# Cross-attention, eight sequences, one core: the queries of batch 2 by seven Strassen products too, weight sums in another order, and parts of GpSimd's work on VectorE and ScalarE

## The chip, the core and the metric

The kernel runs on one core of a Trainium2 chip. The core has five engines that run side by side: TensorE (PE in the profile; its loads of weights are PEld), VectorE (DVE), ScalarE (ACT), GpSimd (POOL) and SyncE (SP), which issues nearly all the transfers. Each engine works through its own list of instructions in order; where one needs another engine's result, it waits on a semaphore, and all that stands behind it on that engine waits too. The metric is the device time of one execution in microseconds.

## The reference

Eight sequences of 256 tokens with 1024 features attend to eight contexts of 256 tokens, with 32 heads of 32 features. Everything is float32, and the mask is all true.

```python
x = (hidden - mu) * rsqrt(var + 1e-5) * gamma + beta     # over the 1024 features
Q = split_heads(x @ Wq.T)
K = V = split_heads(memory)                              # no projection
probs = softmax(where(mask, Q @ K^T * 32 ** -0.5, -inf))
out = hidden + merge_heads(probs @ V) @ Wout.T
```

So there are two large products for each batch, x @ Wq.T and attn @ Wout.T, each of 256 x 1024 by 1024 x 1024, and between them the scores, the softmax and the weighted values of 32 heads.

## The kernel before

**Slots.** The main loop (`for n in range(N)`) has N = 64 passes, called slots here: eight batches of eight groups of four heads. In slot n TensorE computes the scores of group n+1 (`scores`), the values of group n-2 (`values`), a part of the queries of a later batch, and a part of the output projection of the batch before (`project_steps`). In the same slot VectorE, ScalarE and GpSimd work on the softmax of group n+1 (`softmax_parts`). So the first scores instruction of group n+1 marks where slot n begins on TensorE. Slot 4 begins at 50.87 us of the profile, slot 5 at 58.41, slot 6 at 66.17, slot 7 at 73.71, slot 8 at 81.25, slot 9 at 88.79, slot 10 at 96.30 and slot 11 at 103.83.

**The softmax of one group.** For each of four heads, `exps` has VectorE add the mask bias to the scores in PSUM and take the minimum, and ScalarE take the exponential with its sum. Then `normalize` takes the reciprocal of the sum on VectorE and scales the head's 2 x 256 values on GpSimd, `blocks` transposes them in blocks of 32 on VectorE, and `aside` copies two heads' part away on ScalarE for transfers between partitions (pT<-pT and pT<-pc). The order within a slot is written out: exponentials of heads 0, 1, 2, normalize 0, exponentials of 3, copies of queries, normalize 1, a fill, blocks 0, normalize 2, a fill, blocks 1, aside 0, normalize 3, a fill, blocks 2. The last transpose, the second aside and the transfers are the tail; in slots below 7 the tail runs inside the next softmax, after its first exponentials. The scores use four PSUM banks, all of one group, so the scores of group n+1 wait until VectorE has read those of group n.

**Queries.** Direct: `make_q` multiplies eight 128 x 128 blocks of wq by the transposed, normalized x of one batch (256 columns) for each of eight output chunks, and ScalarE copies each result out with the bias. `SPLIT` is the first batch whose queries are computed by seven products of half size instead (Strassen's scheme in Winograd's form): `query_product` does one product a slot, 16 matmuls of 128 columns, in seven of eight slots, and `copy_product` evacuates it on ScalarE (p = 0, 1, 2, 5: four instructions) or VectorE (p = 3, 4, 6). The eighth slot, the one in which the projection does seven steps, has none. The products take sums of quarters of x (`sum_x`, on GpSimd: S1 and S2 two slots before the first product, S4 one before, S3 later) and sums of quarters of wq (`sum_wq`, on GpSimd, made once: T1, T3, T2, T4). T1 to T4 share room with wq itself: some overwrite quarters of it, and T1, B11 and T3 take turns in a small tile, `ring`, which is filled from copies in DRAM (`keep_wq`, `load_ring`, through SP's queue). Before the change SPLIT is 3: batches 0 to 2 are direct.

**x on its way in.** The x of a batch from 2 on is loaded, measured (`ln_stats`: bn_stats, bn_aggr and an addition on VectorE, the power -0.5 on GpSimd), normalized on ScalarE (`ln_norm`), transposed in blocks on VectorE (`blocks_x`) and moved between partitions by sixteen transfers (`move_x`, xnT<-xe). For batch 2 the moves stand in slots 5, 6 and 7; for a later batch whose products begin in slot f they stand in slots f-6, f-5 and f-4. gamma is multiplied into wq, one output chunk a slot (`fold`, GpSimd, slots 0 to 7), since from batch 1 on x is moved without it.

**The projection** (`product_steps`) has seven products too, of four steps each: A11, A12, S2, S3, A22, S1, S4, with sums T1 to T4 of Wout (`sum_wo`, tile wo, on GpSimd). `STEPS` says how many steps stand at three places of each slot. A12 and S2 use the same PSUM bank one after the other (pool ps_o): S2 can begin when VectorE has added A12 to the residual (`store`, row L748), and that addition comes after GpSimd has added p1, the product A11, to the same residual (`add_p1`, row L739). Batch 0 has steps of its own:

```python
if b == 0:
    return STEPS[:1] + ((0, 6, 0), (0, 2, 0), (0, 4, 1), (0, 3, 1)) + STEPS[5:]
return STEPS     # ((0,0,0), (0,7,0), (0,1,2), (0,2,2), (0,2,1), (0,1,2), ...)
```

**GpSimd's order.** What GpSimd does in a slot besides normalizing comes behind it in program order: the power of `ln_stats`, sums for the projection and for x, folds, then the wo and wq sums of the table `sums`.

## Time and profile before

| | us |
|---|---|
| median of 3 runs (571.57 to 572.5) | 572.11 |
| the profiled execution's own time | 571.69 |
| its span in the profile | 569.9 |
| slots 9 to 17 on TensorE (88.79 to 168.66) | 79.87 |
| slots 25 to 33 on TensorE (228.28 to 304.57) | 76.29 |

| group | instructions | mean ns of one |
|---|---|---|
| L533, GpSimd scales half a head's values | 512 | 478 |
| L366, GpSimd multiplies gamma into a chunk of wq | 8 | 1900 |
| L182 and L396, GpSimd makes a quarter of a wo or wq sum | 16 and 16 | 1278 and about 1285 |
| L253, the second half of x 1 normalized on GpSimd | 1 | 3775 |
| L253, other halves of x normalized on VectorE | 2 | 800 |
| L332, moves of x, from issue to landing (50 to 95 us) | 16 | 2000 to 4800, median 3200 |

In the timelines below, the columns are the start in microseconds, the duration, the engine, the line, the operation, the tiles (written<-read), the shape and the number of instructions, and in brackets how long the engine had been idle and what ended the wait. In the groups by form they are the same names, then the busy time of all, the mean duration of one in ns, and the engine's idle time before them. Matmuls overlap, so a group's busy time divided by its number is the price of one, not its mean duration.

### The profile page before, as it was taken

To read this page: it belongs to the slowest core of one execution; us is meant where nothing else is said; L and a number is where in the kernel's file an instruction comes from. 1 tells how busy PE (TensorE), PEld (TensorE's weight loads), DVE (VectorE), ACT (ScalarE), POOL (GpSimd) and SP (SyncE) were. 2 spreads that over 40 slices of the span, in tenths; PEclk is the share of its full clock that TensorE was granted. 3 is DMA by queue.
4 is the path that set the end of the run, shared out by engine and by line. 5 is a ranking of instruction groups with operands and counts; after the bars stand their busy time and mean duration, and the time that the engine had idled before them with its cause. 6 is when DMAs were issued, how large, how long until landed. Compare 5 with 4: busy or idle time off the path is not lost.

```text
span 569.9 us, 20012 instructions
## 1 busy us (share of the span) xinstructions
PE 565.0 (99%) x7170; PEld 393.5 (69%) x7170; DVE 460.1 (81%) x1696; ACT 411.3 (72%) x1426; POOL 413.2 (72%) x679
## 2 busy tenths in 40 slices
PE   9999999999999999999999999999999999999997
PEld 8788786666667677667776777667866767755454
DVE  5888888787877878989898888988888878879823
ACT  4688887777768858787667867778767776769920
POOL 2788899899897896876568576677648657448780
PEclk9999999999999999999999999999999999999999
DMA  8974777656687767877688767896568874436751
GB/s 308 396 194 145 221 198 214 209 163 191 190 254 261 223 182 212 258 219 226 183 244 237 222 170 215 245 281 176 139 180 262 240 212 132 136 110 180 212 164 75
DMA packets 47187, 117.98 MB, mean 207 GB/s; under 512 B 8944, under 2 KB 9712, under 8 KB 47088
## 3 DMA queue, kind: packets, MB, share of 16 engines
q1 hardware_dynamic: 46944, 116.69, 68.8%
q8 instruction: 57, 0.93, 0.7%
q14 instruction: 42, 0.34, 0.2%
q10 hardware_dynamic: 144, 0.01, 0.0%
HBM read 65.28 MB, written 11.53 MB: 135 GB/s over the span
## 4 chain that ended last, share of the span: by engine, by line
PE 90%; POOL 3%; DVE 2%; ACT 2%; issue 1%; DMA 1%; SPq 1%; DVEq 0%; POOLq 0%; ACTq 0%
PE po_S L706 20%; PE pq_A L445 16%; PE pv L620 11%; PE sc L484 11%; PE pq L345 10%; PE po_A L706 10%; PE pq_S L445 6%; PE po_end L773 3%; POOL e L533 2%; ACT e L524 1%; PE po_last L773 1%; PE busy L119 1%; DVE e L520 1%; DMA pT<-pc 1%; POOL wo L182 1%
## 5 line engine op out<-in xcount | busy, mean ns | idle before, releaser
L533 POOL TENSOR_SCALAR e<-e,rden 128x256 f32<-128x256 f32 x512 | 236.0, 478 | 113.3 <-DVE rden L531 110.2
L524 ACT ACTIVATE e<-e,mn 128x256 f32<-128x256 f32 x512 | 254.0, 501 | 48.3 <-DVE mn L520 47.1
L539 DVE STREAM_TRANSPOSE pT<-e 128x512 f32<-128x512 f32 x256 | 180.9, 707 | 45.5 <-POOL e L533 34.8
L520 DVE CUSTOM_DVE_ANT_0 e<-sc,mb 128x256 f32<-128x256 f32 x512 | 185.3, 416 | 27.4 <-PE sc L484 26.8
L545 ACT COPY pc<-pT 128x512 f32<-128x512 f32 x128 | 79.1, 618 | 68.8 <-DVE pT L539 39.3
L524 ACT ACTIVATION_READ_ACCUMULATOR e<-e,mn 128x1 f32 x512 | 97.9, 191 | 0.0
L345 PE MATMUL pq<-xnT,wq 128*128 128x256 f32 (+1 forms) x368 | 84.0, 382 | 0.2 <-ACT qa L354 0.2
L345 PEld LDWEIGHTS pq<-xnT,wq 128*128 128x128 f32 x368 | 68.8, 190 | 14.8 <-issue 4.0
L706 PE MATMUL po_S<-wo,at 128*128 128x512 f32 x152 | 74.5, 607 | 0.4 <-DVE r L748 0.2
L484 PEld LDWEIGHTS sc<-k,qa 32*128 32x128 f32 x1024 | 46.1, 184 | 41.6 <-issue 24.6
L620 PE MATMUL pv<-pT,v 64*32 64x128 f32 x4096 | 74.2, 274 | 0.0
L484 PE MATMUL sc<-k,qa 32*128 32x256 f32 x1024 | 73.6, 400 | 0.1
L620 PEld LDWEIGHTS pv<-pT,v 64*32 64x32 f32 x4096 | 57.0, 105 | 22.5 <-issue 13.1
L706 PE MATMUL po_A<-wo,at 128*128 128x512 f32 x128 | 59.4, 605 | 0.0
L706 PE MATMUL po_S<-wo,s 128*128 128x512 f32 x104 | 49.9, 605 | 0.0
L531 DVE RECIPROCAL rden<-den 128x2 f32<-128x2 f32 x256 | 37.7, 147 | 6.3 <-ACT e L524 5.4
L520 DVE DVE_READ_ACCUMULATOR2_ANT mn<- 128x1 f32 x512 | 42.5, 83 | 0.0
L706 PEld LDWEIGHTS po_A<-wo,at 128*128 128x128 f32 x128 | 22.9, 189 | 25.7 <-issue 24.6
L445 PEld LDWEIGHTS pq_A<-xnT,wq 128*128 128x128 f32 x320 | 37.3, 192 | 4.8 <-issue 4.1
L706 PEld LDWEIGHTS po_S<-wo,at 128*128 128x128 f32 x152 | 25.6, 190 | 20.9 <-issue 19.3
L445 PE MATMUL pq_A<-xnT,wq 128*128 128x128 f32 x320 | 37.3, 275 | 0.0
L739 POOL TENSOR_TENSOR r<-r,p 128x512 f32<-128x512 f32 x24 | 30.7, 1278 | 3.6 <-ACT e L524 2.5
(101 smaller groups left out, 612.1 us busy)
## 6 DMA issues: line engine op xcount, KB each, us to landing
v<-in_kv_dram SPq DMA_DIRECT2D x32, 512.0 KB, 4.3
pT<-pT SPq DMA_DIRECT2D x128, 128.0 KB, 2.4
pT<-pc SPq DMA_DIRECT2D x128, 128.0 KB, 4.2
ring<-kept_T SPq DMA_DIRECT2D x18, 512.0 KB, 5.7
k<-in_kv_dram SPq DMA_DIRECT2D x32, 256.0 KB, 2.9
x<-in_x_dram SPq DMA_DIRECT2D x15, 512.0 KB, 6.1
r<-in_x_dram SPq DMA_DIRECT2D x28, 256.0 KB, 4.4
out_dram<-r SPq DMA_DIRECT2D x28, 256.0 KB, 3.3
```

Source lines behind the costliest of these rows:

```text
L345: nc.tensor.matmul(pqs[n], wq[:, o, c, :], xnTs[b](c), start=(c == 0), stop=(c == NC - 1),)
L445: nc.tensor.matmul(pqs[b][:, o, :], w[:, c], x_[:, c], start=begins and o + c == 0, stop=c == NK - 1, skip_group_check=True,)
L484: nc.tensor.matmul(scs[n][j][:, s, :], qa[r, n % NQ, ts(s, P)], ks[n - n % 2][r, n % 2, :], start=True, stop=True,)
L520: nc.vector.tensor_tensor_reduce(out=e[:, s, :], in0=pss[j][:, s, :], in1=mbs[n // NQ], scale=1.0, scalar=NO_SCORE, op0=ALU.add, op1=ALU.m ...
L524: nc.scalar.activation(e[:, s, :], e[:, s, :], AF.Exp, bias=mn[:, s : s + 1], scale=-1.0, accum_out=den[:, s : s + 1],)
L531: nc.vector.reciprocal(rden, dens[j])
L533: nc.gpsimd.tensor_scalar(es[j][:, s, :], es[j][:, s, :], rden[:, s : s + 1], 1.0, ALU.mult, ALU.mult,)
L539: nc.vector.transpose(pT[:, :, :, j, :, :].rearrange("p a i s k -> p (a i) s k"), es[j].rearrange("p s (b t) -> p b s t", t=K),)
L545: nc.scalar.copy(pc[:, :, ts(j, 2)], pT[:, 1, :, ts(j, 2)])
L620: nc.tensor.matmul(pvs[n][r][j * HD : (j + 1) * HD], vs[n - n % 2][ts(r, 2 * K), i, ds(n % 2 * P + j * HD, HD)], pT[ts(r, 2 * K), :, i, j, ...
L706: nc.tensor.matmul(po, operand(b, name)[:, c], wo[:, which, c], start=begins and c == 0, stop=c == NK - 1, skip_group_check=not begins,)
L739: nc.gpsimd.tensor_tensor(r, r, p1s[b], ALU.add)
```

## The change

SPLIT becomes 2, so batch 2's seven products stand in slots 10 to 16. Batch 0's projection takes the same steps as the other batches. The weight sums of wq are made in slots 6 to 14 in the order T1, T2, T3, T4, with T2 = B22 - T1 and T3 = T2 - B11; T3 is made in `ring` and kept from there. Batch 2's product A11 reads B11 from wq itself. Of GpSimd's work, these parts move: the last head's normalizing of softmaxes 1 to 14 to ScalarE (with its reciprocal and instruction ahead of `blocks(1)`), the second half of x 1 to VectorE, gamma into the second half of wq to VectorE (`fold_late`, eight instructions as fills of slots 4 and 5), and four wo sums and three wq sums to VectorE. The other wo sums stand in earlier slots. The moves of batch 2's x stay in slots 5 to 7.

```diff
--- before.py
+++ after.py
@@ -173,13 +173,13 @@
             wo[:, which, ts(pair, 2)], rows.rearrange("(c p) q -> p c q", c=2)
         )
 
-    def sum_wo(which, c):
+    def sum_wo(which, c, engine=nc.gpsimd):
 
         a, b, op = {
             T3: (B22, B12, ALU.subtract), T2: (T3, B11, ALU.add),
             T4: (B21, T2, ALU.subtract), T1: (B12, B11, ALU.subtract),
         }[which]
-        nc.gpsimd.tensor_tensor(wo[:, which, c], wo[:, a, c], wo[:, b, c], op)
+        engine.tensor_tensor(wo[:, which, c], wo[:, a, c], wo[:, b, c], op)
 
     mks = {}
 
@@ -367,18 +367,25 @@
             wq[:, o], wq[:, o], gs.unsqueeze(2).to_broadcast([P, NC, P]), ALU.mult
         )
 
-    SPLIT = 3
+    def fold_late(*chunks):
+        for c in chunks:
+            nc.vector.tensor_scalar(
+                wq[:, ds(NK, NK), c], wq[:, ds(NK, NK), c], gs[:, c : c + 1], None, ALU.mult
+            )
+    SPLIT = 2
     SOON, LATE = 0, NK
     W_AT = {"B12": (SOON, 0), "B22": (SOON, NK), "B11": (LATE, 0), "B21": (LATE, NK),
-            "T2": (SOON, 0), "T3": (SOON, 0), "T4": (LATE, 0)}
+            "T2": (SOON, 0), "T4": (LATE, 0)}
 
     def weights(name, o):
 
@@ -387,18 +394,18 @@
         first, k = W_AT[name]
         return wq[:, first + o, ds(k, NK)]
 
-    def sum_wq(to, o):
-        to, a, b, op = {
-            "T1": ("ring", "B12", "B11", ALU.subtract), "T3": ("T3", "B22", "B12", ALU.subtract),
-            "T2": ("T2", "T3", "B11", ALU.add), "T4": ("T4", "B21", "T2", ALU.subtract),
+    def sum_wq(to, o, engine=nc.gpsimd):
+        to, a, b = {
+            "T1": ("ring", "B12", "B11"), "T2": ("T2", "B22", "ring"),
+            "T3": ("ring", "T2", "B11"), "T4": ("T4", "B21", "T2"),
         }[to]
-        nc.gpsimd.tensor_tensor(weights(to, o), weights(a, o), weights(b, o), op)
+        engine.tensor_tensor(weights(to, o), weights(a, o), weights(b, o), ALU.subtract)
 
     def keep_wq(name, half):
 
         pair = ts(half, 2)
-        if name == "T1":
+        if name in ("T1", "T3"):
             nc.sync.dma_start(kept[name][:, pair], ring[:, pair].rearrange("p o c q -> p o (c q)"))
         else:
             first, k = W_AT[name]
@@ -436,6 +443,8 @@
 
     def query_product(b, p):
         name, which, begins = Q_PRODUCTS[p]
+        if b == SPLIT and name == "A11":
+            which = "B11"
         if begins:
             pqs[b] = ps_q.tile([P, NK, P], F32, tag="pq", name=f"pq_{b}_{name}")
         x_ = x_part(b, name)
@@ -491,6 +500,7 @@
             pass
 
     tails = []
+    BY_ACT = range(1, 2 * NQ - 1)
 
 
     def softmax_parts(n, copies=(), ahead=(), between=(), hooks={}, fill=()):
@@ -530,6 +540,11 @@
             rden = sm.tile([P, NS], F32, tag="rden", name=f"rden_{n}_{j}")
             nc.vector.reciprocal(rden, dens[j])
             for s in range(NS):
+                if j == NH - 1 and n in BY_ACT:
+                    nc.scalar.activation(
+                        es[j][:, s, :], es[j][:, s, :], AF.Copy, scale=rden[:, s : s + 1]
+                    )
+                    continue
                 nc.gpsimd.tensor_scalar(
                     es[j][:, s, :], es[j][:, s, :], rden[:, s : s + 1], 1.0,
                     ALU.mult, ALU.mult,
@@ -579,9 +594,12 @@
             hook()
         normalize(2)
         fill_in()
+        if n in BY_ACT:
+            normalize(3)
         blocks(1)
         aside(0)
-        normalize(3)
+        if n not in BY_ACT:
+            normalize(3)
         fill_in()
         blocks(2)
         while fill:
@@ -658,8 +676,6 @@
     def steps_of(b):
         if b == B - 2:
             return ENDS
-        if b == 0:
-            return STEPS[:1] + ((0, 6, 0), (0, 2, 0), (0, 4, 1), (0, 3, 1)) + STEPS[5:]
         return STEPS
 
     assert all(sum(map(sum, steps_of(b))) == len(PRODUCTS) * NK for b in range(B - 1))
@@ -810,8 +826,8 @@
             )
         else:
             when = dict(
-                loads=(first - 12, first - 11) if b == SPLIT else (first - 13, first - 12),
-                stats=(first - 10, first - 9) if b == SPLIT else (first - 11, first - 9),
+                loads=(first - 12, first - 11) if b == SPLIT + 1 else (first - 13, first - 12),
+                stats=(first - 10, first - 9) if b == SPLIT + 1 else (first - 11, first - 9),
                 norms=(first - 8, first - 7), trans=(first - 7, first - 6),
                 moves=tuple(first - 6 + (i + 2) // 6 for i in range(16)),
             )
@@ -832,17 +848,20 @@
 
 
     sums = {n: [] for n in range(N)}
-    for n, which, *chunks in (
-        (3, T3, 0), (4, T3, 1), (5, T2, 0), (6, T2, 1), (7, T3, 2), (8, T3, 3), (8, T2, 2),
-        (9, T2, 3), (10, T4, 0), (11, T4, 1, 2), (12, T4, 3), (12, T1, 0), (13, T1, 1, 2),
-        (14, T1, 3),
+    for n, engine, which, *chunks in (
+        (1, nc.gpsimd, T3, 0), (2, nc.gpsimd, T3, 1), (4, nc.gpsimd, T2, 0, 1),
+        (4, nc.gpsimd, T3, 2), (5, nc.gpsimd, T3, 3), (5, nc.gpsimd, T2, 2, 3),
+        (6, nc.gpsimd, T4, 0), (7, nc.gpsimd, T4, 1), (9, nc.vector, T4, 2, 3),
+        (10, nc.vector, T1, 0, 1), (13, nc.gpsimd, T1, 2), (14, nc.gpsimd, T1, 3),
     ):
-        sums[n] += [partial(sum_wo, which, c) for c in chunks]
-    for n, which, *chunks in (
-        (9, "T1", 0), (14, "T1", 1, 2), (15, "T1", 3), (15, "T3", 0), (16, "T3", 1),
-        (17, "T3", 2), (18, "T3", 3), (19, "T2", 0), (20, "T2", 1, 2, 3), (21, "T4", 0, 1), (22, "T4", 2, 3),
+        sums[n] += [partial(sum_wo, which, c, engine) for c in chunks]
+    for n, engine, which, *chunks in (
+        (6, nc.gpsimd, "T1", 0, 1), (7, nc.gpsimd, "T1", 2, 3), (9, nc.gpsimd, "T2", 0, 1),
+        (10, nc.gpsimd, "T2", 2), (11, nc.gpsimd, "T2", 3), (11, nc.gpsimd, "T3", 0),
+        (12, nc.gpsimd, "T3", 1, 2), (13, nc.gpsimd, "T3", 3), (13, nc.vector, "T4", 0),
+        (14, nc.vector, "T4", 1, 2), (14, nc.gpsimd, "T4", 3),
     ):
-        sums[n] += [partial(sum_wq, which, o) for o in chunks]
+        sums[n] += [partial(sum_wq, which, o, engine) for o in chunks]
 
 
     S3_SLOTS = [(b, NQ * b + {0: NQ, 1: NQ - 1}.get(b, NQ - 2)) for b in range(B)]
@@ -850,12 +869,12 @@
 
     away, rings = {n: [] for n in range(N)}, {n: [] for n in range(N)}
     for n, name, half in (
-        (9, "B11", 0), (10, "B11", 1), (15, "T1", 0), (16, "T1", 1), (17, "T3", 0), (19, "T3", 1),
+        (7, "T1", 0), (8, "T1", 1), (9, "B11", 0), (10, "B11", 1), (13, "T3", 0), (14, "T3", 1),
     ):
         away[n].append(partial(keep_wq, name, half))
     for n, b in firsts.items():
         for slots, name in (((n - 3, n - 2), "T1"), ((n, n), "B11"), ((n + 2, n + 2), "T3")):
-            if b > SPLIT or name != "T1":
+            if b > SPLIT:
                 for half, slot in enumerate(slots):
                     rings[slot].append(partial(load_ring, name, half))
 
@@ -893,7 +912,7 @@
     make_q(2)
     for _ in first:
         pass
-    ln_norm(1, 1, nc.gpsimd)
+    ln_norm(1, 1, nc.vector)
 
 
     steps, evacuations = {}, {n: [] for n in range(N + 1)}
@@ -979,6 +998,7 @@
         elif n <= NQ:
             fill = [partial(ln_stats, *args, parts=(i,)) for args in stats[n] for i in range(3)]
             fill += [partial(blocks_x, *args) for args in trans[n]]
+            fill += [partial(fold_late, *chunks) for chunks in {4: ((0, 1), (2, 3), (4, 5)), 5: ((6, 7),)}.get(n, ())]
         if n + 1 < N:
             softmax(n + 1, copies, ahead, between, hooks, fill)
             for q in behind_p1:
@@ -1029,7 +1049,7 @@
             make_q(halves[n], second=True, chunks=range(NC // 2))
         if n == 0:
             nc.gpsimd.tensor_scalar(gs, gam, NEG_SCALE, 1.0, ALU.mult, ALU.mult)
-        if n < NQ:
+        if n < NK:
             fold(n)
         for one in sums[n]:
             one()
```

## The prediction

> **What bounds the kernel now.** I read the page first, then the groups by form, then the timelines of single engines around slots 3 to 12 (slot n is pass n of the main loop; TensorE opens it with the scores of softmax n+1).

> ```profile
> span 569.9 us, 20012 instructions
> ...
> PE 565.0 (99%) x7170; PEld 393.5 (69%) x7170; DVE 460.1 (81%) x1696; ACT 411.3 (72%) x1426; POOL 413.2 (72%) x679
> ```

> TensorE is busy all the time, so less matmul work shortens the run one for one, and every microsecond that TensorE is made to wait lengthens it one for one. The other engines have 19 to 28% to spare over the whole span, but not in each slot. The groups by form price the work that goes and comes:

> ```profile
> L345 PE MATMUL pq<-xnT,wq 128*128 128x256 f32 x256 | 58.1, 381 | 0.2 <-ACT qa L354 0.2
> L445 PE MATMUL pq_A<-xnT,wq 128*128 128x128 f32 x320 | 37.3, 275 | 0.0
> L866 DVE TENSOR_SCALAR x<-x,mv 128x512 f32<-128x512 f32 x1 | 0.5, 478 | 0.0
> ```

> A pass of 256 columns costs 58.1/256 = 0.227 us, one of 128 columns 37.3/320 = 0.117 us. The third row prices a fold on VectorE (512 elements).

> **The gain on TensorE.** Batch 2 has 128 wide passes (29.05 us); seven products are 7 x 32 = 224 narrow ones (26.1 us): 2.95 us less. The order on TensorE in slots 9 to 16 becomes that of slots 25 to 32, which the trace has, and slot 17 becomes slot 33. Scores 26, 34 and 35 start at 228.28, 296.20 and 304.57, so those nine slots take 76.3 us; slots 9 to 17 now take 79.87 (88.79 to 168.66). That is 3.55 us less, 0.4 of it idle time of 0.20 and 0.22 us at two products that goes too. I take 3.5.

> **A bank that is wanted a slot earlier.** With the new step table, S2 of batch 0 starts in slot 10, no longer in slot 11. It needs the bank of A12, which VectorE empties after GpSimd has added p1 to the residual. The TensorE rows of batch 2's projection show when it comes:

> ```profile
> 228.28 1.15 PE L484 MATMUL sc<-k,qa 32*128 32x256 f32 x16
> ...
> 236.64 1.15 PE L484 MATMUL sc<-k,qa 32*128 32x256 f32 x16
> ...
> 238.81 1.13 PE L706 MATMUL po_A<-wo,at 128*128 128x512 f32 x2
> 239.77 2.51 PE L445 MATMUL pq_S<-sx,ring 128*128 128x128 f32 x21
> ```

> The seven-step slot takes 8.36 us; then 3.13 us pass to the product, and a product takes 3.67 (224.61 to 228.28). Slot 9 starts at 88.79, so TensorE wants the bank at 88.79 + 8.36 + 6.80 = 103.95. Before, it was emptied at 105.23 (row at 104.63, itself 1.55 us late because of GpSimd) and wanted at 106.00.

> **The new wait of GpSimd.** In slot 8 GpSimd now adds up S1 of batch 2's x, in the place of two wo sums. All sixteen moves of that x must have landed, and those of slot 7 stand in SP's queue behind softmax 8's transfers:

> ```profile
> 84.07 1.14 SPq L598 DMA_DIRECT2D pT<-pT  x2
> ...
> 87.67 1.24 SPq L602 DMA_DIRECT2D pT<-pc  x2
> 88.96 4.27 SPq L332 DMA_DIRECT2D xnT<-xe  x6
> ```

> ```profile
> 90.55 1.27 POOL L682 TENSOR_TENSOR at<-at 128x512 f32<-128x512 f32 x1
> 91.78 2.50 POOL L182 TENSOR_TENSOR wo<-wo 128x512 f32<-128x512 f32 x2
> 94.26 3.65 POOL L533 TENSOR_SCALAR e<-e,rden 128x256 f32<-128x256 f32 x8
> ```

> The last move starts near 92.6 and lands 2.0 to 4.8 us (median 3.2) after; I take 95.0. GpSimd is there at 91.8, so it waits 3.2 us, and the normalising of softmax 10 is queued behind. Later batches have two slots between last moves and S1; this one has one. On from 95.0 by rows: S1 and S2 sums 2.5 (97.5); three normalisings of 0.92 (100.25); two VectorE transposes of 0.62 (101.5); statistics of x 3, 1.2 and 0.4 (103.1); on GpSimd rstd 0.55, two T2 sums 2.5, the addition of p1 1.25 (107.4); VectorE's emptying add 0.65: 108.1. TensorE waits from 103.95: **+4.15 us**, with nothing else late. Nearest ends for this term: 1.3 if the moves were in time (105.23 as before), 6 if landing takes 4.8 us.

> **What makes the softmax loop later before that.** The normalising of the last head goes to ScalarE, two ACTIVATEs of 128x256 (row L358: 474 ns; a pair of L354 takes 0.82), about 0.75 us in 14 slots. ScalarE has that time: before the transposes' copy and before the next exponentials it waits 0.2 to 1.2 us a slot (0.93 before the row at 62.16). The reciprocal that moves ahead of a transpose on VectorE costs 0.5 us in slots 2 and 3, where it now waits for ScalarE; slot 3's 1.22 us wait of ScalarE for x 2's shift absorbs it. Without that cover it is at most 0.75 us a slot over slots 4 to 8, 3.7. I take nothing; nor a gain, since a turn of the loop by ScalarE's rows (0.50 to its first exponential, eight of 0.49, copies 0.51 and 0.31, reciprocal 0.2, two transposes 1.25: 6.7, three make 7.4) is close to the 7.09, 7.27 and 7.30 that it takes at 61.66 to 83.32.

> The folds of wq's late half are six VectorE ops in slot 4, two in slot 5. GpSimd is spared 4 x 1.9 us, but it is not on the path there.

> ```profile
> 58.10 1.23 DVE L316 STREAM_TRANSPOSE xe<-x 128x1024 f32<-128x1024 f32 x1
> 59.25 0.67 DVE L539 STREAM_TRANSPOSE pT<-e 128x512 f32<-128x512 f32 x1
> ...
> 61.03 0.71 DVE L539 STREAM_TRANSPOSE pT<-e 128x512 f32<-128x512 f32 x1 [0.41 <-POOL e L533]
> 61.66 0.39 DVE L520 CUSTOM_DVE_ANT_0 e<-sc,mb 128x256 f32<-128x256 f32 x1
> ```

> Here VectorE does not wait except those 0.41 us, so 6 x 0.39 us (starts follow 0.09 us before an end) push softmax 6 from 61.66 to 63.75: +2.1. That is the low end. The high end is in rows where a VectorE tensor_scalar meets a GpSimd instruction:

> ```profile
> 10.88 0.29 DVE L474 TENSOR_SCALAR mb<-mk 128x256 f32<-128x256 uint8 x1
> ```

> ```profile
> 279.24 1.27 POOL L682 TENSOR_TENSOR at<-at 128x512 f32<-128x512 f32 x1
> ```

> ```profile
> 280.14 0.51 DVE L474 TENSOR_SCALAR mb<-mk 128x256 f32<-128x256 uint8 x1
> ```

> Alone it takes 0.29 us; beside GpSimd it ends 0.14 us after GpSimd's instruction does (280.65 against 280.51), and so does each of the seven that overlap one. In the new slot 4 three wo sums of 1.27 us run on GpSimd just when four folds come. If every fold waits for one running sum, softmax 6 starts at 66.2, and with the same in slot 5 and at the mask, softmax 8's last copy is 5.1 us late. No row shows what two queued folds do, so I take the middle of 2.1 and 5.1: **+3.6 us**. No slot up to 8 gives it back (turns above), SP's moves shift with it, and so does the 108.1. On the way TensorE would wait first at the scores of slot 6: banks free at about 68.6, wanted at 66.4.

> **Sums on VectorE.** Two wo sums stand in slot 9 right before softmax 11, two in slot 10, three wq sums in 13 and 14 (0.60 us each, by VectorE's adds of that size). They come after the statistics, so they delay the emptying add only if they hold up GpSimd's rstd: 0 to 1.3 us (one sum); row 19.70, an rstd beside a VectorE op, is 1.11 instead of 0.55: I take **+0.3**. [...]

> **At nothing.** ScalarE's sixteen evacuations (0.37 us) and VectorE's three (0.65) fall where batches 3 to 7 have them, in slots in which TensorE shows no idle time. The x 1 half on VectorE (0.8 for GpSimd's 3.8) ends before TensorE's transposes at 27.31. T2, T3, T4 are due in slots 13, 14, 15; the tightest, T3's last quarter, has about 1 us. SP gets two more loads of 0.5 MB and earlier T1 and T3 writes; the sums they wait for are a slot old, TensorE reads the ring at slot 18. If that cover went, 5.7 us of a landing.

> **Sum.** -3.5 + 4.15 + 3.6 + 0.3 = +4.55 us on the profiled 571.69 (span 569.9 and 1.8 around it): 576.2. The median of the runs is 0.4 higher: **576.7**.

> **Rivals.**
> - *No contest on SBUF:* folds cost 2.1 and sums 0: +2.75, 574.9. For it: the row at 6.24, a fold-like op ending in the middle of a GpSimd one. Against: the mask rows.
> - *Strict alternation:* 5.1 and 1.3: +7.05, 579.2.
> - *Other side, a faster loop:* the loop now waits for GpSimd's normalising (1.27 us at 95.23, 0.41, 0.2). With a quarter of it gone each turn of slots 0 to 8 could be 0.5 us shorter; the copy of softmax 8 and the moves behind it then come up to 4 us earlier and cancel folds and bank. It decides from where copy 8 ends before 83.4, 0.65 earlier than now; at its best only part of the bank's 1.3 us stays: 569.9. Against it: ScalarE's chain above.
> - *The products save nothing:* against it, five batches at 0.117 us a pass; with all waits then 580.

> **Chances.** Forecast (waits of 3 to 6 us net) 0.45, strict 0.14, no contest 0.18, faster loop 0.20, no saving 0.03. Within 0.2% (1.1 us, about what this kernel's measurement can tell) falls part of the third and fourth case: of no contest 0.03 there and 0.02 beyond, of the faster loop 0.05 there and 0.15 beyond. Faster 0.17, same 0.08, slower 0.75. Range 570.5 to 579.5; given slower, 574 to 579.5.

> **What will show it.** Nine slots of 76 us less waits; a TensorE wait for VectorE at slot 6's scores and at S2 in slot 10; GpSimd's S1 sum waiting for a DMA; folds longer than 0.48 us. Wrong if the moves land before GpSimd asks, or if softmax 6 starts before 63.

## The result, and the profile after

The changed kernel takes 581.27 us (median of 4 runs, 580.21 to 581.94) against 572.15 us before: a ratio of 1.0159, 95% interval 1.0141 to 1.0176. It is 9.1 us slower. The forecast was 576.7, range 570.5 to 579.5: the direction was right, the size was not, and the time lies above the range.

The profiled execution has a span of 579.6 us, 9.7 more than before (page, first lines):

```profile
span 579.6 us, 20202 instructions
...
PE 569.3 (98%) x7266; PEld 398.5 (69%) x7266; DVE 473.1 (82%) x1715; ACT 423.7 (73%) x1462; POOL 389.5 (67%) x643
```

TensorE is busier by 4.3 us, although its work has become shorter. The slots, from one start of the scores to the next on TensorE's timeline, say where the 9.7 us lie:

| slots | before, us | after, us | difference |
|---|---|---|---|
| up to slot 0's scores | 22.65 | 22.95 | +0.3 |
| 5 | 7.77 | 8.37 | +0.6 |
| 6 | 7.54 | 12.96 | +5.4 |
| 9 to 17 | 79.87 | 82.14 | +2.3 |
| 26 | 8.51 | 9.60 | +1.1 |

Slots 9 to 17 were to become 76.3 us. All of them have the length that batches 3 and later show, but slot 10, which takes 13.55 us and not 8.51, and slot 15 (9.30, not 8.51). So the 3.5 us of the products are there, and 13.3 us have been lost on top. (The start takes 22.4 to 24.0 us in the profiles of this case, so its 0.3 us are not put down to the change.)

TensorE's timeline shows the two places (start, length, instructions, and in brackets the idle time ahead of the group and what ended it):

```profile
67.06 0.69 PE L493 MATMUL sc<-k,qa 32*128 32x256 f32 x2 [0.55 <-DVE mn L530]
68.36 3.51 PE L493 MATMUL sc<-k,qa 32*128 32x256 f32 x14 [0.60 <-DVE mn L530]
71.79 1.96 PE L638 MATMUL pv<-pT,v 64*32 64x128 f32 x64
```

```profile
113.62 3.46 PE L722 MATMUL po_S<-wo,s 128*128 128x512 f32 x4 [3.30 <-DVE r L764]
```

The first are the scores of slot 6, which wait for softmax 6. The second is S2 of batch 0 in slot 10, which waits until VectorE has emptied the bank. But the rows behind the waits are long too: 64 pv matmuls take 1.96 us, elsewhere 1.16; four po_S take 3.46, elsewhere 1.98. The windows of slots 5, 6, 9 and 10 (length, busy time and instructions by engine, granted TensorE clock, DMA share, GB/s) show why:

```profile
58.69:67.06 8.37, 7.65 (x105) 6.09 (x104) 8.37 (x17) 3.98 (x13) 6.11 (x7) 1.00 0.57 174
67.06:80.02 12.96, 12.36 (x104) 9.02 (x105) 11.92 (x47) 11.61 (x43) 10.08 (x16) 0.74 0.64 177
...
95.10:103.47 8.37, 8.37 (x96) 4.19 (x95) 4.03 (x21) 6.30 (x23) 5.11 (x7) 1.00 0.78 235
103.47:117.01 13.54, 10.24 (x119) 6.80 (x118) 11.93 (x38) 8.77 (x30) 13.00 (x18) 0.87 0.65 217
```

In the two slots with a wait the clock is granted at 0.74 and 0.87 on the mean, everywhere else at 1.00, and in the kernel before at 1.00 in every slot. In the trace it is 0.5 for 6.8 us from 68.8 and for 3.4 us from 113.2. A busy TensorE is not a TensorE at its speed here: this is the part of the loss that the prediction did not have.

VectorE's folds (L373, the multiplications by gamma) and GpSimd's wo sums (L182) in slot 5's stretch:

```profile
60.16 1.09 DVE L373 TENSOR_SCALAR wq<-wq,gs 128x512 f32<-128x512 f32 x2
...
61.85 2.66 DVE L373 TENSOR_SCALAR wq<-wq,gs 128x512 f32<-128x512 f32 x2
...
65.06 1.26 DVE L373 TENSOR_SCALAR wq<-wq,gs 128x512 f32<-128x512 f32 x2
66.25 0.41 DVE L530 CUSTOM_DVE_ANT_0 e<-sc,mb 128x256 f32<-128x256 f32 x1
```

```profile
61.55 4.09 POOL L182 TENSOR_TENSOR wo<-wo 128x512 f32<-128x512 f32 x3
```

A pair of folds takes 0.8 us where GpSimd does nothing (shown further down). The pair that meets two sums takes 2.66, and softmax 6 starts at 66.25, where the prediction had 66.2 for strict alternation. GpSimd's S1 sum of x in slot 8, and the wq sums ahead of the addition that frees the bank:

```profile
99.76 1.27 POOL L442 TENSOR_TENSOR sx<-xnT 128x512 f32<-128x512 f32 x1 [3.18 <-DMA xnT<-xe]
...
109.03 2.59 POOL L403 TENSOR_TENSOR wq<-wq,ring 128x512 f32<-128x512 f32 x2
```

It waits 3.18 us for the moves (predicted 3.2).

### The profile page after: what moved, and what is told of

Its sections match the earlier page's. It is cut to its first block, busy times and chain, and to the rows that moved or that the text cites. A ratio compares the mean times of both kernels' runs of the same rounds, so it can differ in the third digit from the quotient of the medians.

```text
span 579.6 us, 20202 instructions
## 1 busy us (share of the span) xinstructions
PE 569.3 (98%) x7266; PEld 398.5 (69%) x7266; DVE 473.1 (82%) x1715; ACT 423.7 (73%) x1462; POOL 389.5 (67%) x643
## 4 chain that ended last, share of the span: by engine, by line
PE 75%; DVE 7%; DMA 5%; POOL 5%; ACT 4%; issue 2%; SPq 2%; POOLq 0%; ACTq 0%; DVEq 0%
PE po_S L722 19%; PE pq_A L454 16%; PE sc L493 10%; PE pv L638 9%; PE po_A L722 8%; PE pq_S L454 6%; ACT e L534 3%; PE po_end L789 3%; DVE pT L554 2%; POOL e L548 2%; DVE e L530 2%; DMA xnT<-xe 2%; DMA pT<-pT 1%; DMA r<-in_x_dram 1%; PE po_last L789 1%
## 5 line engine op out<-in xcount | busy, mean ns | idle before, releaser
L548 POOL TENSOR_SCALAR e<-e,rden 128x256 f32<-128x256 f32 x484 | 225.1, 483 | 139.8 <-DVE rden L541 135.2
L493 PEld LDWEIGHTS sc<-k,qa 32*128 32x128 f32 x1024 | 47.8, 185 | 44.9 <-issue 19.5
L493 PE MATMUL sc<-k,qa 32*128 32x256 f32 x1024 | 76.7, 404 | 1.2 <-DVE mn L530 1.1
L345 PE MATMUL pq<-xnT,wq 128*128 128x256 f32 (+1 forms) x240 | 55.9, 388 | 0.2 <-POOL e L548 0.2
L722 PE MATMUL po_S<-wo,s 128*128 128x512 f32 x104 | 51.8, 623 | 4.1 <-DVE r L764 4.1
L454 PEld LDWEIGHTS pq_A<-xnT,wq 128*128 128x128 f32 x416 | 48.5, 192 | 6.2 <-issue 5.0
L345 PEld LDWEIGHTS pq<-xnT,wq 128*128 128x128 f32 x240 | 45.3, 193 | 8.9 <-issue 1.7
L454 PE MATMUL pq_A<-xnT,wq 128*128 128x128 f32 x416 | 48.5, 275 | 0.0
L541 DVE RECIPROCAL rden<-den 128x2 f32<-128x2 f32 x256 | 38.1, 150 | 11.7 <-ACT e L534 10.6
```

The lines of the kernel that those rows point to most:

```text
L345: nc.tensor.matmul(pqs[n], wq[:, o, c, :], xnTs[b](c), start=(c == 0), stop=(c == NC - 1),)
L454: nc.tensor.matmul(pqs[b][:, o, :], w[:, c], x_[:, c], start=begins and o + c == 0, stop=c == NK - 1, skip_group_check=True,)
L493: nc.tensor.matmul(scs[n][j][:, s, :], qa[r, n % NQ, ts(s, P)], ks[n - n % 2][r, n % 2, :], start=True, stop=True,)
L541: nc.vector.reciprocal(rden, dens[j])
L548: nc.gpsimd.tensor_scalar(es[j][:, s, :], es[j][:, s, :], rden[:, s : s + 1], 1.0, ALU.mult, ALU.mult,)
L722: nc.tensor.matmul(po, operand(b, name)[:, c], wo[:, which, c], start=begins and c == 0, stop=c == NK - 1, skip_group_check=not begins,)
```

## The experiments

The theory: (a) folds against GpSimd's sums stall slot 6, (b) GpSimd standing in front of the moves stalls slot 10, (c) each stall is followed by half clock; ScalarE's normalising is free and the 3.5 us are real. Rivals: ScalarE is too full; the half clock has nothing to do with the stalls; the products save nothing.

### The folds back on GpSimd

```
-   fill += [partial(fold_late, ...)]       # slots 4 and 5
-   if n < NK: fold(n)
+   if n < NQ: fold(n)
+   wo sums: T3 in 1, 2, 3, 3; T2 in 4, 4, 5, 5 (GpSimd); T4 in 9, 9, 10, 10, T1 in 11, 12 (VectorE)
```

> The changed kernel with the folds of the late half of wq back on GpSimd in slots 4 to 7, and with the weight sums spread so that GpSimd has room (wo: T3 in slots 1 to 3, T2 in 4 and 5, T4 on VectorE in 9 and 10, T1's first half on VectorE in 11 and 12). Theory (VectorE's folds alternate with GpSimd's sums, softmax 6 is late, TensorE stalls at slot 6's scores, and its clock is then granted at half for 6.8 us): first exponential of softmax 6 back near 62.0, no TensorE wait for VectorE at slot 6's scores, granted clock 1.0 in slot 6; slot 6 falls from 12.96 to about 7.6 us and slot 5 from 8.37 to 7.8. The wait for S2's bank in slot 10 stays (3 to 4 us, then half clock). Time 581.3 - 5.4 - 0.6 = 575.3 (574.5 to 577). Rival A (the normalising on ScalarE, which is 95 to 100% busy in slots 1 to 8, makes the loop late): the wait at slot 6 stays, 580 to 581. Rival B (the halved clock has nothing to do with the waits and comes by chance): the stall goes, but a half-clock stretch of several us shows up somewhere else or in slot 6 all the same, 578 or more.

Measured: 577.4 us, ratio 1.0091 (1.0076 to 1.0107). Softmax 6 starts 3.25 us behind its scores, as before the change (7.56 in the changed kernel); slots 5 and 6 take 7.76 and 7.54 us at clock 1.00. So (a) is right, and ScalarE (98% busy in slot 5 of this kernel) did not cause that stall. But 2 us of the expected gain are missing, and slots 9, 10 and 11 are 1.1, 1.2 and 0.9 us longer than in the changed kernel:

```profile
91.80 6.28 PE L722 MATMUL po_A<-wo,at 128*128 128x512 f32 x14 [1.08 <-ACT qa L354]
...
109.01 3.78 PE L722 MATMUL po_S<-wo,s 128*128 128x512 f32 x4 [4.14 <-DVE r L764]
```

TensorE arrives earlier, the bank's chain does not: the wait grew from 3.30 to 4.14 us, half clock behind it for 6.8 us.

### Batch 0's old step table, alone and with the folds on GpSimd

```
+   if b == 0:
+       return STEPS[:1] + ((0, 6, 0), (0, 2, 0), (0, 4, 1), (0, 3, 1)) + STEPS[5:]
```

> The changed kernel with batch 0's step table of before (S2 of batch 0 begins in slot 11, not in 10). Theory: the wait for S2's bank in slot 10 (3.30 us) and the half clock behind it go, slot 10 falls from 13.55 to about 8.6 us; slot 6 stays at 13 us. Time 581.3 - 5.0 = 576.3 (575.5 to 577.5). Rival C (the bank's wait only hides a later one: the sums behind GpSimd's wait for the moves are late for a product too): TensorE waits in slot 10 or 11 for something else, 578 to 581.

> Folds on GpSimd with the spread sums, and batch 0's old step table: both of the edits before this one. Theory: both stalls and both half-clock stretches go and what is left is the saving on TensorE, -3.5 us, plus 0.3 at the start, 0.8 in slot 15 and 1.1 in slot 26: 572.1 - 1.3 = 570.8 (569.8 to 571.6), faster than the kernel before by about 0.2%. Rival A: 575 to 577. Rival D (the products save nothing): 573.5 to 574.5.

Measured: 580.56 (1.0126 to 1.0174) and 577.1 us (1.0069 to 1.0102). With S2 in slot 11 little is won: 0.7 us against the changed kernel, 0.3 against the run before. TensorE's and VectorE's rows of the second kernel:

```profile
106.89 3.69 PE L493 MATMUL sc<-k,qa 32*128 32x256 f32 x16 [1.56 <-DVE mn L530]
```

```profile
100.22 0.71 DVE L554 STREAM_TRANSPOSE pT<-e 128x512 f32<-128x512 f32 x1 [4.94 <-POOL e L548]
```

There GpSimd's S1 sum waits 3.86 us for the moves. Softmax 10's normalising is queued behind it, VectorE waits 4.94 us for that, softmax 11 is late, and TensorE stalls at slot 11's scores, again with half clock (6.8 us). So one cause, the late chain behind the moves, shows at the bank, or at the scores where the bank is wanted later.

### ScalarE's normalising alone, in the kernel before

```
+   BY_ACT = range(1, 2 * NQ - 1)       # last head of softmaxes 1 to 14 on ScalarE, as in the change
```

> The kernel before with nothing changed but that ScalarE normalises the last head of softmaxes 1 to 14. Theory (ScalarE has the room): no change, 572.1 (571.5 to 572.7), no new TensorE wait. Rival A (ScalarE's time makes the loop late): TensorE waits at scores in slots 5 to 8, 574 to 577. The faster loop of the prediction: below 571.4, with softmax 8 earlier than before.

Measured: 571.05 us, ratio 0.9977 (0.9968 to 0.9987). It is faster than both kernels, by 1.2 us against the one before (the spans of the profiled executions, 569.3 and 569.9, show half of that). Slots 5, 11 and 15 are 0.16, 0.46 and 0.49 us shorter, slot 9 is 0.39 longer (TensorE waits 0.32 for ScalarE's qa). The rival that blames ScalarE falls, and so does the theory's "no change". The prediction's faster loop is not what gave the gain: it was to make softmax 8 earlier, and softmax 8 starts 2.87 us behind its scores here, 2.30 before. Later ones are earlier: softmax 12 starts 4.15 us behind its scores, 5.07 before.

### The moves in slots 5 and 6

```
-   moves=tuple(5 + (i + 2) // 6 for i in range(16)),
+   moves=tuple(5 + i // 8 for i in range(16)),
```

> The changed kernel with the sixteen moves of batch 2's x in slots 5 and 6 (eight each) in the place of slots 5 to 7. Theory as it stands after the first four runs: GpSimd's S1 sum of x in slot 8 waits for these moves, and what is queued behind it (normalising, S2's chain) makes either S2's bank or the next softmax late; so the remedy is at the moves and not at the step table. GpSimd's wait for DMA before that sum falls from 3.18 us to under 0.3, TensorE's wait for the bank in slot 10 from 3.30 to under 0.6, no half clock in slot 10; slot 6 stays at about 13 us with its half clock. Time 581.3 - 5.0 = 576.3 (575.3 to 577.5). Rival E (the slowness of slots 9 to 11 is VectorE's and GpSimd's load there, not the wait for the moves): slot 10 or 11 still stalls by 2 us or more, 579 to 581.

> The run with the folds on GpSimd and the spread sums, and the moves in slots 5 and 6 as well. Theory: no stall in slot 6, none in slots 10 and 11, granted clock 1.0 throughout; what is left of the losses is 0.3 at the start, up to 1.1 in slot 9 (TensorE waits for ScalarE's qa) and 0.8 in slot 15. Time 572.2 - 3.5 + 0.3 + 0.8 + 0 to 1.1 = 569.8 to 570.9, faster than before. Rival E: 574 or more. Rival D (the products save nothing): 573 to 574.4.

Measured, alone and with the first run's edits: 579.93 (1.0114 to 1.0162) and 576.8 us (1.0047 to 1.0101). GpSimd no longer waits for the moves, and yet a stall came, in slot 9, which takes 14.03 and 14.82 us. SP's queue, VectorE and TensorE in the second kernel:

```profile
68.21 6.08 SPq L332 DMA_DIRECT2D xnT<-xe  x8
...
77.87 5.33 SPq L332 DMA_DIRECT2D xnT<-xe  x8
...
85.13 0.45 SPq L129 DMA_DIRECT2D x<-in_x_dram  x1
```

```profile
90.49 0.69 DVE L227 BATCH_NORM_STATS2 st<-x 128x6 f32<-128x512 f32 x1 [2.41 <-DMA x<-in_x_dram]
```

```profile
94.73 9.16 PE L722 MATMUL po_A<-wo,at 128*128 128x512 f32 x14 [2.12 <-ACT qa L354]
```

Eight moves fill SP's queue, batch 3's x is loaded late behind them, VectorE stands at its statistics, and q is copied late. That queue had no room for two more moves a slot. The first of the two kernels shows something else. Slot 6 has the very stall of the changed kernel, but the clock stays 1.00:

```profile
68.19 2.56 PE L493 MATMUL sc<-k,qa 32*128 32x256 f32 x14 [0.60 <-DVE mn L530]
70.69 1.16 PE L638 MATMUL pv<-pT,v 64*32 64x128 f32 x64
```

Its slot 6 takes 10.25 us, in place of 12.96: the half clock is worth 2.7 us there.

### The folds on VectorE, without GpSimd's sums beside them

```
+   wo sums: T3 in 1, 2, 3, 3; T2 in 5, 5, 5, 6 (GpSimd): none in slot 4; moves in slots 5 and 6
+   T4 in 9, 9, 10, 10, T1 in 11, 12 (VectorE)
```

> The run with the early moves, the folds on VectorE as in the changed kernel, but GpSimd's three wo sums taken out of slot 4 (two T3 sums in slot 3, three T2 sums in slot 5, the last T2 sum in slot 6, T4 on VectorE in 9 and 10, T1's first half on VectorE in 11 and 12), so that the folds meet a GpSimd that only normalises. Theory (strict alternation of VectorE's folds with GpSimd's sums costs 2.5 us, the folds' own work 2.1): the pairs of folds that took 2.66 us take 0.8 to 1.3, softmax 6's first exponential is at 63.5 to 64.2 and not at 66.25, TensorE waits at most 1.3 us at slot 6's scores, and its clock stays 1.0. Time 570.3 + 1.0 = 571.3 (570.3 to 573). Rival F (the folds are slow for a reason of their own, such as their strided tile): softmax 6 at 65.5 or later, half clock in slot 6, 575 to 577.

Measured: 578.7 us (1.0090 to 1.0135), since the early moves bring their stall of slot 9 again. For the folds the rows decide:

```profile
62.08 0.83 DVE L373 TENSOR_SCALAR wq<-wq,gs 128x512 f32<-128x512 f32 x2
...
63.47 0.83 DVE L373 TENSOR_SCALAR wq<-wq,gs 128x512 f32<-128x512 f32 x2
64.23 0.41 DVE L530 CUSTOM_DVE_ANT_0 e<-sc,mb 128x256 f32<-128x256 f32 x1
```

The first exponential comes 5.32 us behind the scores. With the folds on GpSimd it was 3.25, with VectorE's folds beside GpSimd's sums 7.56: the folds' own work is 2.07 us, the alternation 2.24. Slot 6 takes 8.62 us at clock 1.00.

### Four stalls in the kernel before

```
+   for _ in range({22: 9, 30: 11, 38: 13, 46: 17}.get(n, 0)):
+       nc.vector.bn_stats(gs[:, :6], wo[:, B11, 0])
```

> The kernel before with useless VectorE work behind the softmax of slots 22, 30, 38 and 46 (9, 11, 13 and 17 statistics of 512 elements, some 5.3, 6.5, 7.7 and 10 us), which have 4.45 us of room before TensorE's scores and are alike otherwise: four stalls of rising length at the scores, 0.9, 2.0, 3.2 and 5.6 us in all. Theory (a stall of about 2 us and more has the clock granted at half for 3.4 or 6.8 us behind it, one of 1 us has not): clock 1.0 in slot 23, about 0.5 for 3 to 7 us in slots 31, 39 and 47. Time 572.2 + 11.7 + 3 times 1.7 to 3.4: 589 to 594. Rival B (the halved clock has nothing to do with the waits): clock 1.0 after all four, 584. The output stays that of the reference: the statistics are written to a tile that nothing reads any more.

Measured: 610.9 us, 38.8 more than before. The stalls are longer than expected, and come not at the scores but at the bank that VectorE empties: 5.20, 6.15, 7.62 and 10.53 us.

```profile
225.31 3.78 PE L706 MATMUL po_S<-wo,at 128*128 128x512 f32 x4 [5.20 <-DVE r L748]
```

The slots with the stalls and those just behind them are 38.8 us longer in the profile too. The waits are 29.5 us of that. The other 9.3, some 2.3 us a stall, go with the clock: 0.5 for 6.8, 6.8, 6.8 and 13.7 us, each beginning in a stall, and 1.0 in all the rest. So stalls cause the half clock; that no dose was short enough to be spared it leaves the smallest one open.

### The sums of x a slot later

```
    # slot 8: S1 and S2 sums of batch 2's x  ->  slot 9, behind softmax 10's normalising
+   if slot == n + 1 and firsts[slot] == SPLIT:
+       sum_x(SPLIT, "S1"); sum_x(SPLIT, "S2")
```

> The changed kernel with one edit: GpSimd's S1 and S2 sums of batch 2's x in slot 9, behind the normalising of softmax 10, in the place of slot 8. Theory (GpSimd standing in front of the moves, with softmax 10's normalising queued behind it, is what makes S2's chain late, not its length): the wait before the S1 sum falls from 3.18 us to under 1, softmax 10's last transpose and the exponentials of softmax 11 come some 2.5 us earlier, TensorE's wait for S2's bank in slot 10 falls from 3.30 us to 1 or less, the clock there stays 1.0; slot 6 keeps its stall. Time 581.3 - 5 + up to 1 = 576.3 to 577.3 where slot 6 is followed by 6.8 us of half clock as in the changed kernel, less where it is not. Rival H (the chain of GpSimd's own work between the normalising and p1's addition is too long for slot 10 by itself): the wait for the bank stays above 2 us, 579 to 581.

Measured: 578.58 us (1.0083 to 1.0123). GpSimd does not wait for the moves any more. TensorE's wait for the bank falls from 3.30 to 2.01 us, no further, and has 3.4 us of half clock behind it. VectorE's and TensorE's rows:

```profile
104.71 2.75 DVE L182 TENSOR_TENSOR wo<-wo 128x512 f32<-128x512 f32 x2
```

```profile
112.35 2.93 PE L722 MATMUL po_S<-wo,s 128*128 128x512 f32 x4 [2.01 <-DVE r L764]
```

Two T4 sums take 2.75 us beside GpSimd's sums (1.28 with none beside them), and then stand in front of softmax 11. Theory and rival H are both half right.

### A version with the waits taken out, and three more on it

```
    # folds on GpSimd, wo sums as in the first run, sums of x in slot 9, (e9)
    #   wq sums: T1 in 6, 7, 8, 8, T2 in 10, 10, 11, 11, two of T4 on GpSimd in 14
    # e15: e9, batch 1's last q copied ahead of ScalarE's normalising (n <= NQ + 1)
    # e11: e15, VectorE's T4 of wo in 10, 10, 11, 11, T1 in 12, 13; GpSimd all late T4 quarters of wq
    # e12: e11 with the old step table
```

> A version aimed at beating both kernels: the changed kernel with the folds of the late half on GpSimd in slots 4 to 7, the wo sums spread as in the first run, the two sums of batch 2's x moved from slot 8 to slot 9 (behind softmax 10's normalising, so that GpSimd does not stand in front of the moves), the wq sums one to three slots later where their deadline allows (T1 in slots 6, 7 and 8, T2 in 10 and 11, two of T4 on GpSimd in slot 14). Theory (all that the change loses are waits behind contested folds and behind the moves, each with a half-clock stretch; the products save 3.5 us and ScalarE's normalising 0.6 to 1.2): softmax 6 at 3.25 us behind its scores, GpSimd's wait for the moves under 1.2 us, no TensorE wait above 0.6 us in slots 6 to 16, granted clock 1.0 throughout, time 572.2 - 3.5 + 0.3 + 0.2 to 1.0 = 569.2 to 570.2, faster than before. Rival G (ScalarE's and GpSimd's load in slots 6 to 10 is the bound, whatever the order): TensorE stalls for qa or the scores in slots 8 to 11, 573 or more.

> The version with the waits out and one more edit, the copy of batch 1's last q ahead of ScalarE's normalising of the last head in slot 8: TensorE's wait of 1.06 us for ScalarE's qa in slot 9 falls to 0.3 or less. If the waits add up: 574.45 - 0.9 = 573.5. If the gain is only handed on to the next wait (S2's bank in slot 10, 2.20 us, whose chain does not depend on TensorE): that wait grows to about 3.2 us and the time stays at 574.3.

> The version with the waits out once more, with its four remaining TensorE waits taken at their cause: VectorE's two T4 sums of wo leave slot 9 (they took 3.19 us beside GpSimd's sums in the place of 1.28, and stood in front of softmax 11 and of the addition that frees S2's bank) for slots 10 and 11, T1's for 12 and 13; the copy of batch 1's last q goes ahead of ScalarE's normalising in slot 8; T3's last quarter goes ahead of wo's sum in slot 13; T4's three late quarters are all GpSimd's in slot 14. Theory (two-input sums on VectorE and GpSimd serialise, so what was moved to VectorE was not taken off the path, only put in front of the softmax): TensorE's waits of 1.06 (slot 9), 2.20 (slot 10), 0.95 (slot 14) and 0.74 us (slot 15) fall to 0.6 or less each, 1.5 in all, clock 1.0 throughout; time 574.45 - 3.5 (2.5 to 4.5) = 571 (569.9 to 572). Rival G (the engines' load in slots 6 to 14 is the bound): the waits move to other places, and the time stays at 573.5 or more.

> The same with batch 0's step table of before, S2 in slot 11. Theory: with the front of the wait gone, the later start of S2 is now worth what is left of the wait for its bank, 0 to 1 us, and costs nothing: 570.5 (569.5 to 572). If instead the old table's denser slot 11 makes GpSimd or VectorE late there, 572 or more.

Measured: 574.45 (1.0022 to 1.0045), 574.37 (1.0027 to 1.0057), 578.11 (1.0089 to 1.0123) and 576.87 us (1.0074 to 1.0104). The first wins 6.8 of the 9.1 us back, with clock 1.00 in the profile, but it lies some 4 us above the expected range and is not faster than the kernel before, and four waits of 4.7 us in all are left:

```profile
91.82 6.28 PE L722 MATMUL po_A<-wo,at 128*128 128x512 f32 x14 [1.06 <-ACT qa L354]
107.08 1.98 PE L722 MATMUL po_S<-wo,s 128*128 128x512 f32 x4 [2.20 <-DVE r L764]
...
141.47 1.16 PE L454 MATMUL pq_A<-sx,ring 128*128 128x128 f32 x8 [0.66 <-POOL ring L403]
...
153.10 1.98 PE L722 MATMUL po_S<-wo,at 128*128 128x512 f32 x4 [0.74 <-DVE r L764]
```

The second kernel removes the wait for qa in slot 9 altogether, and the time stays:

```profile
107.44 1.98 PE L722 MATMUL po_S<-wo,s 128*128 128x512 f32 x4 [3.15 <-DVE r L764]
```

1.06 us less in slot 9 are 0.95 more in slot 10, because the bank's chain does not depend on TensorE. In the third and fourth the sums moved to later slots make waits of 2.50 (with 3.4 us of half clock behind it) and 2.48 us for the bank in slot 14, and of 1.28 and 2.77 for a wo sum in slot 15. As the rival said, the waits only move.

### VectorE's sums left out, or replaced

```
    # e15, T4 of wo zeroed at the start, and in sum_wo and sum_wq:
+   if engine is nc.vector: return                                        # e13
+   if engine is nc.vector: nc.vector.bn_stats(gs[:, :6], wo[:, a, c]); return   # e14 (sum_wq: wo[:, 0, o])
```

> The version with the waits out, with the copy of batch 1's last q ahead of ScalarE's normalising in slot 8, and with VectorE's weight sums left out (the six of wo and the two of wq that it still had; so T4, half of T1 and two quarters of wq's T4 are not computed and the output is not the reference's; T4 of wo is set to zero at the start so that it can be read). Theory (what is left of the loss are VectorE's sums that run against GpSimd's two-input sums): TensorE's waits in slots 9 (1.06), 10 (2.20), 14 (0.95) and 15 (0.74) fall to 0.6 in all, time 574.45 - 4.4 = 570 (569.3 to 571); then the products' saving of 3.5 us is real and was only eaten. Rival G2 (GpSimd alone is too full in slots 9 to 14, VectorE has nothing to do with it): waits of 2 us and more stay, 572 to 574.

> The same, but with each of VectorE's weight sums replaced by a statistics instruction over 512 elements (0.58 to 0.68 us, about what the sum takes alone, with one SBUF input; it was never longer beside GpSimd in these traces); the same sums are left uncomputed. Theory (the price is the alternation with GpSimd, not VectorE's own time): nearly as fast as without them, 570.5 (569.5 to 571.7), statistics at 0.58 to 0.7 us each, GpSimd's sums at 1.27 and not 1.7. Rival I (VectorE's time itself is what is missing): as slow as with the sums, 572.8 to 574.

Measured: 570.96 (0.9963 to 0.9991) and 571.82 us (0.9980 to 1.0003). Both kernels leave out VectorE's eight weight sums, so they do not compute the reference and only show what those sums cost. In slots 6 to 17 one wait of more than 0.2 us is left, 1.34 and 1.36 us for the bank in slot 10. VectorE's statistics in the place of the sums, GpSimd's sums beside them, and TensorE, in the second kernel:

```profile
101.95 1.41 DVE L184 BATCH_NORM_STATS2 gs<-wo 128x6 f32<-128x512 f32 x2
110.06 1.38 DVE L184 BATCH_NORM_STATS2 gs<-wo 128x6 f32<-128x512 f32 x2
```

```profile
110.21 2.53 POOL L410 TENSOR_TENSOR wq<-wq,ring 128x512 f32<-128x512 f32 x2
```

```profile
106.82 1.98 PE L729 MATMUL po_S<-wo,s 128*128 128x512 f32 x4 [1.36 <-DVE r L771]
```

With the sums (first of the four kernels above), the same two pairs took 3.19 and 2.42 us on VectorE, and GpSimd's pair 3.40:

```profile
100.41 3.19 DVE L182 TENSOR_TENSOR wo<-wo 128x512 f32<-128x512 f32 x2
110.33 2.42 DVE L182 TENSOR_TENSOR wo<-wo 128x512 f32<-128x512 f32 x2
```

So it is not VectorE's time that is missing: the same time spent on statistics costs 0.9 us in all (571.82 against 570.96), on sums with two SBUF inputs 3.4 (574.37). In the kernel without the sums, slots 9 to 17 take 78.08 us, 10.25 of them slot 10 with its last wait; without that it is 76.3, the figure of the prediction. The products do save 3.5 us.

## Why the prediction was right or wrong, point by point

**The gain on TensorE (-3.5): right**, in the changed kernel and without VectorE's sums (76.3 us).

**Folds (+3.6): right in kind, low in size.** The stall is where it was forecast, and softmax 6 starts at the time given for strict alternation, not at the middle that I took. Slots 5 and 6 lost 6.0 us. 2.7 of them are half clock (12.96 against 10.25 us behind the same stall), which leaves 3.3 for the wait, near the 3.6 taken. That is luck in part, since 3.6 was the middle between two cases, and the folds did what the higher one said.

**The bank of S2 (+4.15): right in kind.** GpSimd's wait was 3.18 us (3.2 forecast). TensorE waited 3.30, and slot 10 lost 5.04: four po_S at half clock are 1.48 of it.

**Sums on VectorE (+0.3): too low.** Slot 15 lost 0.8 us behind two sums of 2.36 us. The runs show what such sums, with two SBUF inputs, cost: 1.28 us a pair with no sum of GpSimd's beside it, up to 3.19 beside GpSimd's sums, and no such growth for statistics with one input (1.41 and 1.38 us a pair beside them).

**The step that failed** is the pricing of both wait terms. The prediction says that every microsecond that TensorE is made to wait lengthens the run one for one, and enters a wait with the time that TensorE idles. The clock behind it is missing, 2.7 + 1.5 = 4.2 us. That is most of the 5.2 us between the sum's 576.2 and the profiled 581.4; the others are 1.1 in slot 26, 0.5 in slot 15 (beyond the 0.3 taken) and 0.3 at the start, less 0.9 where the two waits were a little shorter than taken. The kernel before has no half clock after its start (1.00 from 6.79 us to 569.8), and no wait of TensorE in slots 5 to 17 above 0.22 us, so its trace could not show the price. The runs show half clock behind the wait of 3.30 us at the bank and behind gaps of 0.55 and 0.60 us and smaller ones at the scores, and at the bank behind waits down to 2.01 us.

**At nothing.** ScalarE's normalising was taken at neither gain nor loss; alone it gains 0.2%, but in slots 11 and 15, and not by the faster loop up to slot 8 that the rival had. Its cost is elsewhere: with the folds on GpSimd, TensorE waits 1.06 us for ScalarE's qa in slot 9; that wait is gone in the kernel with the copy ahead of the normalising. Slot 26's 1.1 us (GpSimd waits 3.46 us for r, whose load SP issued late) was not foreseen, and all other profiles have that slot at 8.51: what made it late in this execution is open.

**The terms do not add.** Taking out the folds (expected -6.0 us) gave -3.9, the old step table (-5.0) gave -0.7, both together -4.2. The waits hang on one chain, from the moves over GpSimd to softmax 11 and the bank, and TensorE's arrival only decides which shows.

## What to carry to other kernels

Price a wait of a dense TensorE at its idle time plus the half-clock stretch that may follow (3.41 and 6.83 us long in the changed kernel, worth 1.48 and 2.7 us), and compare variants over several runs, since the same stall has it in one kernel and not in another. Moving two-input sums from GpSimd to VectorE takes less off a busy GpSimd than it seems: beside GpSimd's own sums the two hold each other up (2.53 us of GpSimd's became 3.40, 1.28 of VectorE's up to 3.19), and on VectorE they stand in front of the softmax; where VectorE has to be given work, give it some that the rows show untouched, such as the statistics here (0.65 to 0.70 us each beside GpSimd's sums). Before work is moved ahead by eight slots, look whether each queue on its way (SP's too) has room in those slots: here the products' 3.5 us are real, but in none of the orders tried did the sums that they need fit before slot 15, and of the complete kernels measured only the one with the smallest part of the change is faster than before.

## What the runs showed of the hardware

```profile
109.83:113.25 3.42, 1.41 (x7) 0.81 (x6) 1.94 (x9) 2.43 (x10) 3.42 (x6) 1.00 0.84 294
113.25:116.66 3.41, 3.41 (x16) 1.56 (x17) 3.12 (x7) 3.29 (x9) 3.41 (x6) 0.50 0.18 71
```

```profile
102.68:106.10 3.42, 1.61 (x15) 1.42 (x13) 3.42 (x15) 1.70 (x7) 2.94 (x3) 1.00 0.88 295
106.10:109.51 3.41, 2.07 (x8) 0.84 (x12) 2.72 (x12) 3.17 (x14) 2.89 (x7) 1.00 1.01 373
```

- In slot 6 of the changed kernel 6.83 us of half clock came behind waits of 0.55 and 0.60 us at the scores. There the rows show less idle time than is lost: behind such a wait 14 scores take 2.56 us at full clock, in the kernel with early moves, where 16 take 1.15 elsewhere.
- No run varied when a stall comes and nothing else, so what decides on the half clock is open.
- The times of one kernel spread with it: four runs of the kernel with folds on GpSimd and early moves took 574.67 us at a mean clock of 1.000, and 576.27 to 577.96 at 0.994 to 0.996.
- VectorE's folds with one SBUF input take turns with GpSimd's sums (0.8 us a pair alone, 2.66 beside them), statistics do not (0.65 to 0.70 us each). So it is not the number of inputs alone.
